# Last block of a linear attention: its scores taken ahead of the values of the block before, a moved root, and a 22nd weight buffer

## Chip, core and metric

One core of a Trainium2 chip runs the whole program. The metric is the device time in microseconds (us), the median over the executions shown; lower is better. Times inside the program are counted from the start of the profiled execution's span. All data is 32-bit floating point.

## What is computed

An input of 4 images, 128 channels, 64 x 64 positions passes two layers; each adds its result to the input. Layer 0 is an attention between all positions of an image (three fifths of the time; the change does not touch it). Layer 1 sees each image as 4096 tokens of 128 numbers, and has two parts:

```python
# attention that runs along the tokens: 8 heads of 128
kv = silu(einsum('btd,ed->bte', layernorm(t), W_kv));  k, v = kv[..., 0], kv[..., 1]
s  = einsum('hd,bthd->bth', q_proj, k)
m  = cummax(s, axis=1);  e = exp(s - m)
t  = t + (cumsum(e[..., None] * v, axis=1) / cumsum(e, axis=1)[..., None]).mean(axis=2)

# 64 experts, each of which chooses 8 tokens of each image
g = layernorm(t);  p = softmax(g @ gate_w.T + gate_b, axis=1)
topv, topi = top_k(p over the tokens, 8)            # for each expert
pooled = sum_k(topv * g[topi])
out = gelu(pooled @ weight1 + b1) @ weight2 + b2     # 64 pairs of matrices
t[topi] += out * topv
```

The experts' two weight arrays are the program's largest input: 64 units of 512 KB, that is one unit for every two experts in each of the two layers of the expert network.

## The kernel before, in words

Layer 1 goes over 32 blocks of 512 tokens (`NB = 32`; 8 blocks an image, 4 chunks of 128 tokens a block). The function `loop` (L1133) walks the blocks and issues, for block n:

- `keys` (L357): the keys of block n+1, eight matmuls into PSUM and eight Silu on ScalarE (L364, L365);
- `gate_stats` (L1002): mean and variance of the finished tokens of block n-1, on VectorE (L87, L88);
- `weights` (L898): transposes of the block's exponentials `es` (L902), a copy of them on ScalarE (L904), and on GpSimd their product with a triangular mask, in two halves `em` (L917); `weighted` (L924) then multiplies the halves with the inverse sums `rb` on VectorE (L926);
- `values` (L929): eight matmuls with the value weights `wvs` (L938) and eight Silu (L942);
- `gate_logits` (L1027), for an earlier block: a matmul `pl` (L1031), a copy with the bias on ScalarE (L1035) and the block's eight largest on VectorE (L1038, the `best()` of the code);
- `gate_norm` (L1007), for block n-1: a square root on ScalarE (L91), a reciprocal (L92), four normalisations (L96). `gate_turn` (L1020) later transposes these (L1023) and copies them (L1025);
- `totals` (L946): matmuls into `pt` (L954) and eight running additions into `before` on VectorE (L964);
- `score` (L835): the scores of block n+1, 16 matmuls (L839); `scan` (L845): two copies (L851), the running maximum (L856), a subtraction (L860), the exponential on ScalarE (L861), a copy of it on GpSimd (L866), the running sum (L871) and its reciprocal (L876); `spread` (L879): the reciprocal goes to DRAM and comes back spread over the partitions as `rb`, by six DMAs on SP's queue (L884, L891);
- `outputs` (L966): 128 matmul pairs into `po` (L974), 16 more with `before` and the reciprocal (L981), and the addition into the tokens `t` (L986).

TensorE's order is the order of this code, written out by hand (`manual_schedule`). The other engines' order is set by a scheduler at build time; `issue_after` holds an instruction behind another one there. Every engine then works off its own list in that order.

For the last block (n = 31, `not more`) there are no further keys or scores. There `gate_norm(30)` stands at the start of the block and runs on VectorE, `gate_turn(30)` and `gate_logits(30)` follow within the block.

After the loop comes the expert part, from L1219. The last block is normalised and its logits are made, the best tokens are chosen and pooled (L1315 to L1360), and then 16 groups of four experts run: `first` (L1362, matmuls L1367), `turn` (L1376), `second` (L1391, matmuls L1397), `gather`. At its end the results are added to `t` (L1480, L1487) and written (L1490).

The weights come through `load_units` (L1238), all on SP's queue. `NW = 21` units fit in at once: thirteen in a pool `fw` that is opened when the loop's buffers are closed, six in `room` (which held keys and transposed tokens), one each in `wks` and `wvs` (the key and value weights). Unit n lies in buffer n mod NW. The first 21 are issued as soon as their buffers are free; after that `first` and `second` issue two units each, into the buffers which they have just read. Two tiles of the gate, `xg` (L1010, normalised tokens) and `xt2` (L1024, their transpose), 2 KB a partition each, are in no unit's list.

Of the kernel before, what the change touches and what calls it, by code (L numbers as in the profile page):

```python
# [13 lines left out]
P = 128  # L14
# [4 lines left out]
def conv_attn_hybrid_kernel(  # L19
# [763 lines left out]
    GRP = BLK // H2  # L783
    EG = E // QG
    NB = B * NBLK
    NW = 21

    def layer1(pre, ready):

# [5 lines left out]
        with ExitStack() as kept, ExitStack() as l1:  # L795
# [46 lines left out]
                    )  # L842
                return pss

            def scan(n, pss):  # L845

                k = n % NBLK
                ss = sb.tile([P, BLK], F32, tag="ss", name=f"{pre}ss_{n}", bufs=1)
                for q in range(NPAIR):
                    half = bass.ts(q, BLK // NPAIR)  # L850
                    nc.vector.tensor_copy(  # L851
                        ss[:, half].rearrange("h (u s j) -> h s u j", u=2, s=2),
                        pss[:, half].rearrange("h (s u j) -> h s u j", u=2, s=2),
                    )
                mm = sb.tile([P, BLK], F32, tag="mm", name=f"{pre}mm_{n}", bufs=1)
                nc.vector.tensor_tensor_scan(  # L856
                    out=mm, data0=ss, data1=ss, op0=ALU.max, op1=ALU.max,
                    initial=state[:, 0:1] if k else LOWEST,
                )
                nc.vector.tensor_sub(ss, ss, mm)  # L860
                exp = nc.scalar.activation(ss, ss, AF.Exp).ins  # L861
                nc.gpsimd.tensor_copy(state[:, 0:1], mm[:, BLK - 1 : BLK])
                es = sb.tile([P, BLK], F32, tag="es", name=f"{pre}es_{n}")
                for q in range(NPAIR):
                    half = bass.ts(q, BLK // NPAIR)
                    nc.gpsimd.tensor_copy(  # L866
                        es[:, half].rearrange("h (s u j) -> h s u j", u=2, s=2),
                        ss[:, half].rearrange("h (u s j) -> h s u j", u=2, s=2),
                    )
                rr = sb.tile([P, BLK], F32, tag="rr", name=f"{pre}rr_{n}")  # L870
                nc.vector.tensor_tensor_scan(  # L871
                    out=rr, data0=ones.to_broadcast([P, BLK]), data1=ss,
                    op0=ALU.mult, op1=ALU.add, initial=state[:, 1:2] if k else 0.0,
                )
                nc.vector.tensor_copy(state[:, 1:2], rr[:, BLK - 1 : BLK])
                inverse = nc.vector.reciprocal(rr, rr).ins  # L876
                return es, rr, (exp, inverse)
# [68 lines left out]
            def totals(n, vs):  # L946

                pt = ps_t.tile([P, 2, GRP // 2, C], F32, tag="t", name=f"{pre}pt_{n}")
                for i, v in enumerate(vs):
                    for h in range(NH):  # L950
                        g, r = h % QG, h // QG
                        for u in range(2):
                            half = slice(u * H2, (u + 1) * H2)
                            nc.tensor.matmul(  # L954
                                pt[g * QW : (g + 1) * QW, u, i, :], ew[half, i, h, :], v[half, h, :],
                                start=(i == 0 and r == 0), stop=(r == NR - 1), skip_group_check=True,
                            )
                if n % NBLK == 0:
                    nc.vector.memset(before[:, 0, :], 0.0)
                else:  # L960
                    nc.vector.tensor_copy(before[:, 0, :], before[:, GRP, :])
                for x in range(GRP):
                    q, u, s = x // 4, x // 2 % 2, x % 2
                    nc.vector.tensor_add(before[:, x + 1, :], before[:, x, :], pt[:, u, 2 * q + s, :])  # L964

            def outputs(n, rr, aas, vs):  # L966
                po = ps_o.tile([P, 2, BLK], F32, tag="o", name=f"{pre}po_{n}")
# [29 lines left out]
            rden = lgp.tile([P, B // 2], F32, tag="rden", name=f"{pre}rden")  # L997

            total = lgp.tile([P, C], F32, tag="total", name=f"{pre}total")
            gmv, grs, xgs, gate_xts, picks, eighth, cts, lefts = {}, {}, {}, {}, {}, {}, {}, {}  # L1000

            def gate_stats(n):  # L1002
# [4 lines left out]
            def gate_norm(n, engine):  # L1007
                grs[n] = gp.tile([P, CPB], F32, tag="grs", name=f"{pre}grs_{n}", bufs=2)
                root = roots(grs[n], gmv[n])
                xgs[n] = gp.tile([P, CPB, C], F32, tag="xg", name=f"{pre}xg_{n}")  # L1010
                for c in range(CPB):
                    normalise(
                        engine, xgs[n][:, c, :], n * CPB + c, gmv[n][:, c, 0:1],
                        grs[n][:, c : c + 1],
                    )

                nc.gpsimd.tensor_copy(rs1[:, bass.ts(n, CPB)], grs[n])
                return root

            def gate_turn(n, ps):  # L1020
                ptr = ps.tile([P, CPB, P], F32, tag="kv", name=f"{pre}gtr_{n}")
                for c in range(CPB):
                    nc.tensor.transpose(ptr[:, c, :], xgs[n][:, c, :], ident)  # L1023
                gate_xts[n] = gp.tile([P, BLK], F32, tag="xt2", name=f"{pre}xt2_{n}")  # L1024
                nc.scalar.copy(gate_xts[n], ptr.rearrange("p c x -> p (c x)"))  # L1025

            def gate_logits(n, ps):  # L1027
# [105 lines left out]
            def loop():  # L1133
# [8 lines left out]
                for n in range(NB):  # L1142
# [2 lines left out]
                        ks = keys(n + 1, xt_of[n + 1], range(NH // 2), kss, ps_kv, pre)  # L1145
                    if n >= 1:
                        gate_stats(n - 1)
                    if not more:
                        gate_norm(n - 1, nc.vector)
                    if n + 2 < NB:  # L1150
                        xls = tokens(n + 2, xl_place)
                    if n == 0:
# [15 lines left out]
                    with ExitStack() as order:  # L1168
                        if k0 == 0:
                            with tc.issue_after(made[2][1]):  # L1170
                                order.enter_context(tc.issue_after(select(0)))
                        if 0 <= k0 < NBLK:
                            left = gp.tile([P, BLK], F32, tag="left", name=f"{pre}left_0_{k0}")
                            marked = pick_mark(0, k0, left)
                            if marked is not None:
                                order.enter_context(tc.issue_after(marked))
                        if 1 <= k0 <= NBLK:
                            order.enter_context(tc.issue_after(pick_turn(0, k0 - 1, ps_kv)))
                        if k0 == NBLK:
                            divisors(0)  # L1180
                        aas = weighted(ems, rbs)
                    vs, last = values(n, xt_of[n])
                    if n >= 2:
                        best = gate_logits(n - 2, ps_kv)
                    if not more:
                        gate_turn(n - 1, ps_kv)
                    if 1 <= k0 <= NBLK:
                        pick_add(0, k0 - 1)
                    with tc.issue_after(last):
                        if n >= 1 and more:  # L1190
                            gate_norm(n - 1, nc.gpsimd)
                        if n == 0 and ready:
                            roots(rs1[:, bass.ts(B - 1, NCH)], mv1[:, bass.ts(B - 1, NCH), :])
                    if n + 2 < NB:
                        copied[n + 2] = turned(n + 2, xls, xt_of[n + 2], ps_kv, pre)
                    totals(n, vs)
                    if not more:
                        best()
                        best = gate_logits(n - 1, ps_kv)
                    if more:  # L1200
                        pss = score(n + 1, ks)
                        with ExitStack() as order:
                            if 0 <= k0 < NBLK:
                                with tc.issue_after(copied[n + 2]):
                                    exp = pick_exp(0, k0)
                                order.enter_context(tc.issue_after(exp))
                            made = scan(n + 1, pss)
                        rbs = spread(n + 1, made[1])
                        if 0 <= k0 < NBLK:
                            with tc.issue_after(made[2][1]):  # L1210
                                pick_keep(0, k0)
                    outputs(n, rr, aas, vs)
                    if n >= 2:
                        best()

# [2 lines left out]

            l1.close()  # L1219
            pool = opener(l1, pre)  # L1220
            fwp = pool("fw", NW - 2 - ROOM)
            fo = pool("l2fo")
            fs = pool("l2fs", 2)
            ps_a = pool("l2a", 4, space=PSUM)
# [13 lines left out]
            def load_units(m):  # L1238
                for _ in range(m):
# [1 line left out]
                    if n >= len(units):  # L1241
                        return

                    if n % NW >= NW - 2:
                        w = wvs if n % NW == NW - 1 else wks.rearrange("d h e -> d (h e)")
                    elif n % NW >= NW - 2 - ROOM:
                        w = room[:, n % NW - (NW - 2 - ROOM), :]
                    else:
                        w = fwp.tile([P, FH + FC * C], F32, tag="fw", name=f"{pre}fw_{n}")
                    nc.sync.dma_start(out=w, in_=fw[units[n][0], units[n][1]])  # L1250
# [3 lines left out]
                w = unit_weights[layer, e // 2].rearrange("p (i x) -> p i x", i=2)[:, e % 2, :]  # L1254
                return w.rearrange("p (c o) -> p c o", c=FC) if layer else w

            load_units(NW)

            eos = fo.tile([P, B // 2, C], F32, tag="eo", name=f"{pre}eo")

# [29 lines left out]
            with tc.manual_schedule(engines={mybir.EngineType.PE}):  # L1290
# [25 lines left out]
                pool_tokens(0, total)  # L1316
                backs(2, nc.vector)
                best = gate_logits(NB - 1, ps_a)
                with tc.issue_after(copied[pre, NB - 1]):
                    backs(2, nc.scalar)  # L1320
                best()
# [233 lines left out]
```

## Time and profile before

| what | us |
|---|---|
| time, median of 3 runs | 2385.71 (2385.66 to 2388.26) |
| the profiled execution: its own time | 2384.92 |
| its span | 2383.2 |
| layer 0's last large matmul, L608 | starts 1444.4 |
| one block of the loop near its end (keys of 30 to keys of 31, 2187.48 to 2212.56) | 25.1 |
| last block's addition into the tokens, L986 | starts 2263.22 |
| first expert matmul, L1367 | starts 2289.87 |
| last unit of weights issued, L1250 | 2341.36 |
| first results ready to write | 2356.5 |

Busy shares of the span: TensorE 98%, VectorE 63%, ScalarE 51%, GpSimd 13%. These are averages over stages that have different limits. From the second of 40 slices of the span to about 2230 us TensorE is busy nearly without a break; in the last 150 us, where the change lies, it waits again and again, and the profile's timeline has to be read there row by row. Such a row gives the start, the time, the engine, the line, the operation, what it writes and reads, the tile's size and the count; in square brackets stands how long the engine had been idle before it and what ended this. The span is cut into 40 slices in the page's second part; the last three are the end of the loop and the experts:

```profile
ACT  5444444444443444443443335666666666666541
DMA packets 61765, 109.93 MB, mean 46 GB/s; under 512 B 10096, under 2 KB 35184, under 8 KB 61552
```

The first line is ScalarE's busy share in tenths by slice; the second sums the DMAs. A third of all bytes, 33.6 MB, are the 64 units of weights.

### The profile page before, as it was taken

What the parts mean: (1) busy time and instruction counts of PE and PEld (TensorE: products, weight loads), DVE (VectorE), ACT (ScalarE), POOL (GpSimd) and SP (SyncE); (2) the same over time, 40 slices, a digit from 0 to 9 for tenths busy, and PEclk for the clock granted to TensorE, in tenths of its full rate; (3) what the DMA queues carried; (4) which work ended last, traced back from release to release, by engine and by line L of the source; (5) the groups of instructions that cost most, each with busy time, mean ns of one, the idle gap of its engine ahead of it and who ended that gap; (6) DMA issues with size and microseconds to landing.
All of it is one profiled execution on the core that took longest, in us unless ns stands there. A gap on an engine that the chain in (4) does not pass through costs nothing.

```text
span 2383.2 us, 45629 instructions
## 1 busy us (share of the span) xinstructions
PE 2340.1 (98%) x19416; PEld 1554.0 (65%) x19416; DVE 1494.8 (63%) x2593; ACT 1208.1 (51%) x1639; POOL 304.2 (13%) x338
## 2 busy tenths in 40 slices
PE   7999999999999999999999999999999999999897
PEld 3567777677778677778777775555555555655554
DVE  6666666666656666655555556666666677776655
ACT  5444444444443444443443335666666666666541
POOL 0000000000000000000000002333343333333300
PEclk9999999999999999999999999999999999999999
DMA  3200110000100000020000000212112121112388
GB/s 83 75 23 19 41 39 1 17 13 23 49 25 1 23 7 23 18 52 1 1 1 1 1 1 19 55 38 55 38 38 55 38 54 39 38 38 55 118 307 322
DMA packets 61765, 109.93 MB, mean 46 GB/s; under 512 B 10096, under 2 KB 35184, under 8 KB 61552
## 3 DMA queue, kind: packets, MB, share of 16 engines
q1 hardware_dynamic: 57824, 101.22, 14.8%
q10 hardware_dynamic: 3728, 5.71, 0.7%
q8 instruction: 154, 2.52, 0.4%
q14 instruction: 59, 0.48, 0.1%
HBM read 85.40 MB, written 8.91 MB: 40 GB/s over the span
## 4 chain that ended last, share of the span: by engine, by line


## 5 line engine op out<-in xcount | busy, mean ns | idle before, releaser
L608 PE MATMUL av<-pr,am 64*128 64x512 f32 x4096 | 1057.2, 591 | 0.0
L587 ACT ACTIVATE pr<-sc 128x1024 f32<-128x1024 f32 x512 | 523.8, 1023 | 675.4 <-PE sc L583 606.7
L590 DVE TENSOR_TENSOR acc<-acc,pr 128x1024 f32<-128x1024 f32 x480 | 587.0, 1223 | 436.0 <-ACT pr L587 435.9
L608 PEld LDWEIGHTS av<-pr,am 64*128 64x128 f32 x4096 | 634.6, 187 | 260.4 <-issue 45.2
L583 PE MATMUL sc<-e,e 64*128 64x512 f32 x2048 | 618.9, 594 | 1.9 <-DMA e<-ee 1.9
L583 PEld LDWEIGHTS sc<-e,e 64*128 64x128 f32 x2048 | 317.3, 188 | 106.5 <-issue 19.5
L364 PE MATMUL pk<-room,wks 128*128 128x512 f32 x508 | 238.3, 607 | 2.0 <-ACT room L365 1.7
L938 PE MATMUL pv<-wvs,room 128*128 128x512 f32 x512 | 227.0, 596 | 2.5 <-ACT v L942 2.1
L942 ACT ACTIVATE v<-pv 128x512 f32<-128x512 f32 x256 | 152.7, 597 | 69.7 <-PE pv L938 69.7
L938 PEld LDWEIGHTS pv<-wvs,room 128*128 128x128 f32 x512 | 97.0, 191 | 121.9 <-issue 114.2
L926 DVE TENSOR_TENSOR em<-em,rb 128x1024 f32<-128x1024 f32 x64 | 78.4, 1224 | 154.4 <-DMA rb<-rd 154.4
L828 POOL MEMSET ew<- 128x1024 f32 x1 | 1.0, 952 | 1360.9 <-PE av L608 1360.9
L365 ACT ACTIVATE room<-pk 128x512 f32<-128x512 f32 x254 | 146.8, 597 | 54.4 <-PE pk L364 54.2
L364 PEld LDWEIGHTS pk<-room,wks 128*128 128x128 f32 x508 | 89.4, 189 | 107.6 <-issue 79.0
L917 POOL TENSOR_TENSOR em<-et,mask 128x1024 f32<-128x1024 f32 x64 | 122.6, 1937 | 79.0 <-ACT et L904 79.0
L96 POOL TENSOR_SCALAR xg<-t,gmv,grs 128x128 f32<-128x128 f32 x120 | 95.2, 806 | 287.3 <-DVE grs L92 209.4
L974 PEld LDWEIGHTS po<-v,em 64*64 64x64 f32 x4096 | 111.6, 133 | 29.1 <-DVE before L964 26.7
L974 PE MATMUL po<-v,em 64*64 64x128 f32 x4096 | 119.9, 271 | 1.9 <-issue 1.9
L876 DVE RECIPROCAL rr<-rr 128x512 f32<-128x512 f32 x32 | 107.3, 3353 | 1.1
L861 ACT ACT_TABLE_LOAD x24 | 30.8, 1283 | 121.1 <-DVE ss L860 121.1
L964 DVE TENSOR_TENSOR before<-before,pt 128x128 f32<-128x128 f32 x256 | 72.6, 284 | 9.6 <-PE pt L954 3.8
L871 DVE TENSOR_TENSOR_SCAN rr<-ones,state,ss 128x512 f32<-128x512 f32 x28 | 42.0, 1501 | 48.7 <-ACT ss L861 46.6
(203 smaller groups left out, 2031.5 us busy)
## 6 DMA issues: line engine op xcount, KB each, us to landing
rb<-rd SPq DMA_DIRECT2D x128, 256.0 KB
fw<-in_fw_dram SPq DMA_DIRECT2D x40, 512.0 KB
room<-in_fw_dram SPq DMA_DIRECT2D x18, 512.0 KB
t<-in_xtok_dram SPq DMA_DIRECT2D x32, 256.0 KB
e<-ee SPq DMA_DIRECT2D x63, 128.0 KB
x<-in_x_dram SPq DMA_DIRECT2D x12, 512.0 KB
e<-ee SPq DMA_DIRECT2D x63, 64.0 KB
out_dram<-t SPq DMA_DIRECT2D x8, 256.0 KB
```

Of the source, the lines that this page charges most:

```text
L96: i = engine.tensor_scalar(out=dst, in0=t[:, chunk, :], scalar1=mean, scalar2=rs, op0=ALU.subtract, op1=ALU.mult)
L364: nc.tensor.matmul(pk, wks[:, h, :], xt, start=True, stop=True)
L365: nc.scalar.activation(kss[h], pk, AF.Silu)
L583: nc.tensor.matmul(sc[:, u, :], e2[halves[u], p, :], e1[halves[u], :], start=True, stop=True)
L587: nc.scalar.activation(pr, sc, AF.Exp)
L590: added.append(nc.vector.tensor_add(acc, acc, pr).ins)
L608: nc.tensor.matmul(av, am[h, j, :], pr[h, u, :], start=(j == 0), stop=(j == NCH - 1))
L876: inverse = nc.vector.reciprocal(rr, rr).ins
L917: nc.gpsimd.tensor_tensor(em, eq.unsqueeze(2).to_broadcast([P, 2 * NH, H2]), mask.unsqueeze(1).to_broadcast([P, 2 * NH, H2]), ALU.mult,)
L938: nc.tensor.matmul(pv.rearrange("p h d -> p (h d)"), xt[:, bass.ts(2 * q + s, P)], wvs[:, bass.ts(m, BLK)], start=True, stop=True,)
L942: last = nc.scalar.activation(v[:, bass.ts(m, HPB), :], pv, AF.Silu).ins
L974: nc.tensor.matmul(po[s * H2 : (s + 1) * H2, u, q, :], aas[q][half, s, h, :], vs[2 * q + s][half, h, :], start=(q == 0 and h == 0), stop=F ...
```

## The change

Six edits, all in layer 1:

1. In iteration 30 the scores of block 31 are issued ahead of the values of block 30 (before: behind its totals).
2. In that iteration `scan` holds the exponential behind the last Silu of the values, and the running sum behind the last of the eight additions of `totals`.
3. In the last iteration `gate_norm(30)` is issued behind the last Silu of that block's own values; `gate_turn(30)` behind `totals`; `gate_logits(30)` behind `outputs`.
4. `xg` and `xt2` become the two halves of one tile, `gate_room` (4 KB a partition, as much as both had).
5. `NW` is 22: `gate_room` is the 22nd buffer. The pool `fw` keeps thirteen.
6. 21 units are issued at first as before; the 22nd, into `gate_room`, behind the logits of block 31.

```diff
-    NW = 21
+    NW = 22
...
-            def scan(n, pss):
+            def scan(n, pss, behind=()):
...
-                exp = nc.scalar.activation(ss, ss, AF.Exp).ins
+                with ExitStack() as order:
+                    for i in behind[:1]:
+                        order.enter_context(tc.issue_after(i))
+                    exp = nc.scalar.activation(ss, ss, AF.Exp).ins
...
+                with ExitStack() as order:
+                    for i in behind[1:]:
+                        order.enter_context(tc.issue_after(i))
+                    nc.vector.tensor_tensor_scan(
...
+            gate_room = gp.tile([P, 2 * BLK], F32, tag="gate_room", name=f"{pre}gate_room")
...
-                xgs[n] = gp.tile([P, CPB, C], F32, tag="xg", name=f"{pre}xg_{n}")
+                xgs[n] = gate_room[:, :BLK].rearrange("p (c d) -> p c d", c=CPB)
...
-                gate_xts[n] = gp.tile([P, BLK], F32, tag="xt2", name=f"{pre}xt2_{n}")
+                gate_xts[n] = gate_room[:, BLK:]
...
-                    if not more:
-                        gate_norm(n - 1, nc.vector)
...
+                    sooner = n + 2 == NB
+                    if sooner:
+                        pss = score(n + 1, ks)
                     vs, last = values(n, xt_of[n])
                     if n >= 2:
                         best = gate_logits(n - 2, ps_kv)
-                    if not more:
-                        gate_turn(n - 1, ps_kv)
...
                     with tc.issue_after(last):
                         if n >= 1 and more:
                             gate_norm(n - 1, nc.gpsimd)
+                        if not more:
+                            gate_norm(n - 1, nc.vector)
...
-                    totals(n, vs)
+                    added = totals(n, vs)
                     if not more:
+                        gate_turn(n - 1, ps_kv)
                         best()
-                        best = gate_logits(n - 1, ps_kv)
                     if more:
-                        pss = score(n + 1, ks)
+                        if not sooner:
+                            pss = score(n + 1, ks)
...
-                            made = scan(n + 1, pss)
+                            made = scan(n + 1, pss, (last, added) if sooner else ())
...
                     outputs(n, rr, aas, vs)
+                    if not more:
+                        best = gate_logits(n - 1, ps_kv)
...
-            fwp = pool("fw", NW - 2 - ROOM)
+            fwp = pool("fw", NW - 3 - ROOM)
...
+                    part = n % NW - (NW - 3 - ROOM)
+                    if part >= 0:
+                        w = (
+                            *(room[:, i, :] for i in range(ROOM)),
+                            wks.rearrange("d h e -> d (h e)"), wvs, gate_room,
+                        )[part]
...
-            load_units(NW)
+            load_units(NW - 1)
...
                 best = gate_logits(NB - 1, ps_a)
+                load_units(1)
```

## Prediction

> **What bounds the kernel now.** I read the busy rows first: TensorE is at nine tenths nearly to the end, but such an average hides single waits, and the edits reorder the last 150 us alone. There I read the timeline row by row, then the waits of SP's queue, then stretches. The timeline, 2230 to 2264 and at the first expert matmul:
>
> ```profile
> 2230.43 1.92 PE L839 MATMUL ps<-room,qz 128*32 128x512 f32 x16
> ...
> 2237.65 0.63 ACT L861 ACTIVATE ss<-ss 128x512 f32<-128x512 f32 x1
> ...
> 2240.04 3.35 DVE L876 RECIPROCAL rr<-rr 128x512 f32<-128x512 f32 x1
> ...
> 2243.56 1.28 ACT L91 ACT_TABLE_LOAD   x1
> ...
> 2245.91 0.30 ACT L91 ACTIVATE grs<-gmv,eps 128x4 f32<-128x4 f32 x1 [1.07 <-DVE gmv L88]
> 2246.23 1.28 ACT L942 ACT_TABLE_LOAD   x1
> ...
> 2248.17 3.70 PE L938 MATMUL pv<-wvs,room 128*128 128x512 f32 x8 [2.10 <-ACT v L942]
> ...
> 2250.88 1.23 DVE L926 TENSOR_TENSOR em<-em,rb 128x1024 f32<-128x1024 f32 x1 [3.20 <-DMA rb<-rd]
> ...
> 2254.21 1.23 DVE L926 TENSOR_TENSOR em<-em,rb 128x1024 f32<-128x1024 f32 x1
> ...
> 2258.85 3.27 PE L974 MATMUL po<-v,em 64*64 64x128 f32 x108 [1.86 <-issue]
> ...
> 2263.22 0.69 DVE L986 TENSOR_TENSOR t<-t,po 128x512 f32<-128x512 f32 x1 [4.62 <-PE po L981]
> ...
> 2289.87 1.04 PE L1367 MATMUL ph<-fw,pooled 128*4 128x512 f32 x8 [0.43 <-DVE pooled L1302]
> ```
>
> To be seen: the scores of block 31 end at 2232.35; a chain over VectorE, exponential, running sum, reciprocal and the trip through DRAM gives `em` only at 2254 and 2255.4; meanwhile ScalarE breaks off its Silus for a square root (two table loads round 2245.91). From L986 to the first expert matmul is a serial 26.65 us. From there the weights decide. SP's waits and two stretches (TensorE, PEld, VectorE, ScalarE, GpSimd busy, clock, DMA share, GB/s):
>
> ```profile
> SPq L1250 <- PE ph L1367: 20.1, 5, 16.3
> ...
> 2280.00:2290.00 10.00, 8.45 (x113) 6.62 (x113) 6.59 (x15) 2.70 (x5) 0.00 (x0) 1.00 0.13 50
> 2310.00:2320.00 10.00, 10.00 (x130) 6.11 (x129) 5.00 (x13) 5.05 (x14) 0.00 (x0) 1.00 1.03 406
> ```
>
> 21 units are loaded, the queue then waits 16.3 us for the first expert matmul, and from about 2300 to 2350 it runs at its ceiling of some 406 GB/s. At the end TensorE waits for `room` and `wks` (1.9, 1.1 and 1.1 us in the view of waits). So the end is set by (a) when the first expert matmul runs and (b) how many units are left then.
>
> **The change part by part**, against the profiled execution (2384.92 us, span 2383.2; the median is 0.79 above it). Times from here lack the leading 22.
>
> *Scores ahead (edits 1, 2).* 16 matmuls held TensorE from 30.43 to the next block of work at 32.28: 1.85. Moved to 20.65 they delay `values(30)` by that; the last Silu ends at 30.1, not 28.3. The last key's Silu ends at 21.45, when the seventh score would start, so it costs 0.2 at most. `po(30)` starts at 32.2 as before: what was behind it is now ahead, cost nothing. Gained: VectorE does L851, L856, L860 between 22.6 and 29.6, in the wait for `rb` (its second copy lies behind `em_0`, whose `rb` lands at 25.8). ScalarE, after the Silu at 30.1: table load 1.28, root 0.30, logits 0.68, table load 1.28, exponential 0.63, with gaps 34.4 instead of 38.28. On VectorE the eight additions follow the logits' maximum: 33.2 to 35.7 (8 x 0.316). Then running sum 1.50, reciprocal 3.35: done at 40.8, before 43.39, **2.6 earlier**. GpSimd has the four normalisations (3.13) first, until 35.5, so `es` is copied at 35.5 to 37.2, not 38.34 to 40.01.
>
> *The values of block 31 (edit 3).* TensorE finishes L981 at 37.0 and finds the exponentials almost there: transposes done 37.7, `et` 37.9, copy and table load to 40.1, first Silu 40.1 (before 42.94). Now no root interrupts: Silus 2 and 3 at once, then one each 0.86: last one ends at 46.0, before 52.51. Here the Trainium skill ("ScalarE: Activation LUTs", What ACT_TABLE_LOAD costs) puts a switch of tables at about 2.66 us, load and drain; the rows show 1.28 and no drain (43.56 + 1.28 = 44.84, root at 45.91 for want of variances). By the page the two switches removed are 5.3, by the rows 2.6 plus the 1.07 wait plus the root. I use the rows. Either way it isn't the sum: `values` is no longer what is late.
>
> *What is late next.* `em_1`. In block 30 it started 10.0 after the reciprocal's end (18.44 to 28.47): 40.8 + 10.0 = 50.8, ends 52.05 (before 55.44). The built order puts `em_0`, three normalisations, `em_1`, the fourth on VectorE (0.26 to 0.34 each), so the fourth ends at 52.4. `gate_turn(30)` is new ahead of `po`: TensorE waits for that fourth and starts `po` at 52.6. Additions of block 31: 52.9 to 55.5, hidden behind `po`. In the old trace `po` restarted at 58.85 with 108 of 128 and L986 came 4.37 later; all 128 take 0.59 more: L986 at 52.6 + 4.96 = 57.6, **5.6 earlier**. The old 1.86 of "issue" goes too: it came 3 us after `totals`, with weights in flight; now 4 us of waiting lie between, enough to fetch code.
>
> *The clock, which speaks against it.* `totals(31)` end at 48.1 and `po` starts at 52.6: TensorE does three transposes in 4.5 us. What that does, two stretches of the old trace (busy TensorE, clock, DMA share, GB/s) show:
>
> ```profile
> 2237.38:2240.79 3.41, 1.16 (x9) 1.00 0.32 126
> 2240.79:2244.20 3.41, 3.41 (x7) 0.50 0.00 0
> ```
>
> A stretch of 3.41 with 1.16 busy is followed by one at half the clock. The skill ("TensorE: Matmul & The Clock Gate", Part 1) says at least one idle window of about 3.4 us is needed, free-running; its table "Why this matters for your kernels" asks for "No PE-idle gaps >~3µs between matmul bursts". By the page's wording I would charge nothing unless a whole window falls into the gap; by the row a third busy is enough, so I charge it: on average some 2 us of `po` at half speed, **1.0 lost** (0 to 1.8). L986 then at 58.6, 4.6 earlier.
>
> *The tail.* `gate_logits(30)` now follows `po`: its two matmuls fit into the 0.75 between L981's end and the transposes of `t`. But on ScalarE its copy (0.68) and the seed stand ahead of the copies of transposes, and the next root waits for those: **0.4 later** (0 to 0.7). The table load at L1309 (1.28) goes; it was in ScalarE's slack.
>
> *Weights (edits 4 to 6).* The 13 `fw` loads start with L981's end and move with it. The 22nd follows them, 1.28 of transfer at about 76, in the queue's idle time before the first expert matmul at about 85.7: hidden. After that 42 units remain instead of 43, each freed buffer comes one unit earlier, and units land 1.28 apart in the stretch at the ceiling: **1.28 earlier**, as TensorE's waits there (4.1 us) exceed it. One tile in place of two adds waits to each normalisation of GpSimd, for its own work and TensorE's of a block ago, 20 us past: nothing. If these were late, GpSimd's queue (`es`, `em`) would pay; it is idle half of each block. SP's queue keeps its order around `rd` and `rb`; four `room` units and `wks` now start at 23.3 rather than 31.6, behind `rb(30)`, and are done by about 35, ahead of `rd(31)` at 40.8.
>
> Sum: -4.6 + 0.4 - 1.3 = **-5.5**; 2384.9 - 5.5 = 2379.4 in an execution like the profiled one, and from the median 2385.7 - 5.5 = **2380.2 us**.
>
> **Rivals.**
>
> *Most is given back (no measurable change).* A starved TensorE: weights now flow from 23 to 35, under `totals(30)` and `po(30)`, as they did under `po(31)` when it stood 2 us on "issue". One such stop at `po(30)` costs the path little (values have 2 us of slack against `em`), but a second in `po(31)`, 2.1, with the clock's 1.8 leaves 5.6 - 2.1 - 1.8 - 0.4 + 1.3 = 2.6: 2383.1. For it: that row. Against: `po(31)` is reached later after `totals` than before.
>
> *The 22nd unit brings nothing*, because the experts are bound by TensorE: 2381.5. Against it are the 4.1 us of waits for weights.
>
> *Slower.* One mechanism: code for TensorE held up by weights, at each of the four crossings between 30 and 58 plus one in the tail's transposes. Each is 2.1; three eat 6.4 of the 6.9 that the steps gain without the clock, so it decides from the fourth on the path: five with the clock's 1.0 and 0.4 for the tail give 2385.7 + 10.5 + 1.4 - 6.9 = 2390.7. Against: block 30 had 3.5 us of weights in flight at `po` without a stop.
>
> *It doesn't do what it says*: the built lists show each move, so only the sizes are open.
>
> **How the numbers follow.** Forecast, with gains between 4.8 and 8: 0.63. Given back: 0.23. No 22nd unit: 0.10 (half of it still past the bound, with less clock loss). Slower: 0.04. A difference under 0.2%, 4.8 us, is about what can't be told from none. So faster 0.68, same 0.28, slower 0.04. Range: below, no clock loss and no tail loss give 2378.8, and a selection that escapes the half clock which the old trace has at 2274.9 about 1 more, 2377.7; above, the first rival, 2383.1.
>
> **What would show it.** The exponential of block 31 near 34.4, no table load among the last Silus, their end at 46, L986 at 57.6 to 59, the first expert matmul at 84.5 to 86, the load into `gate_room` inside the idle stretch, the last unit issued near 2335.5. Wrong if `rb` of block 31 lands later than 10 us after its reciprocal, if `po(30)` shows "issue" and drags `es`, or if the clock is at half all through `po(31)`.

## The result, and the profile after

| | before | after |
|---|---|---|
| time, median of 8 executions each, same chip | 2386.1 (2384.91 to 2388.26) | 2380.34 (2377.78 to 2382.02) |
| ratio | | 0.9975, 95% interval 0.9966 to 0.9985 |
| the profiled execution's own time | 2384.92 | 2380.49 |
| first `rd` of block 30 issued (L884, now L892) | 2218.47 | 2217.95 |
| last block's addition into the tokens (L986, now L997) | 2263.22 | 2259.74 |
| first expert matmul (L1367, now L1389) | 2289.87 | 2286.61 |
| last unit of weights issued | 2341.36 | 2336.81 |

The changed kernel is faster: 5.8 us in the medians, 4.4 between the two profiled executions (4.5 in their spans). The latter splits into stages: L997 comes 3.48 earlier, the way from there to the first expert matmul is 0.22 longer, the stretch from that to the last unit is 1.29 shorter, and behind it nothing changes (41.83 and 41.86 to the end of the span). But 0.52 of the 3.48 was there already at the first `rd` of block 30, before the first edit acts (2218.47 and 2217.95 in the table); from there on L997 is 2.96 earlier. The timeline of the changed kernel, the rows that answer to those of before:

```profile
2233.47 0.63 ACT L866 ACTIVATE ss<-ss 128x512 f32<-128x512 f32 x1
...
2234.93 1.96 PE L985 MATMUL po<-v,em 64*64 64x128 f32 x59 [0.79 <-issue]
...
2237.07 3.35 DVE L884 RECIPROCAL rr<-rr 128x512 f32<-128x512 f32 x1
...
2240.93 1.57 ACT L950 ACTIVATE v<-pv 128x512 f32<-128x512 f32 x3
...
2246.17 0.60 ACT L950 ACTIVATE v<-pv 128x512 f32<-128x512 f32 x1 [0.26 <-PE pv L946]
...
2246.79 1.28 ACT L91 ACT_TABLE_LOAD   x1
...
2247.81 1.23 DVE L934 TENSOR_TENSOR em<-em,rb 128x1024 f32<-128x1024 f32 x1 [4.00 <-DMA rb<-rd]
...
2248.08 0.30 ACT L91 ACTIVATE grs<-gmv,eps 128x4 f32<-128x4 f32 x1
...
2250.04 1.23 DVE L934 TENSOR_TENSOR em<-em,rb 128x1024 f32<-128x1024 f32 x1
...
2251.57 0.33 PE L1036 MATMUL gtr<-ident,gate_room 128*128 128x128 f32 x1 [1.10 <-DVE gate_room L96]
...
2251.83 0.88 PE L985 MATMUL po<-v,em 64*64 64x128 f32 x22
...
2253.71 4.93 PE L985 MATMUL po<-v,em 64*64 64x128 f32 x106 [0.99 <-issue]
...
2259.74 0.69 DVE L997 TENSOR_TENSOR t<-t,po 128x512 f32<-128x512 f32 x1 [4.93 <-PE po L992]
...
2270.88 0.33 SPq L1271 DMA_DIRECT2D gate_room<-in_fw_dram  x1
...
2286.61 1.04 PE L1389 MATMUL ph<-fw,pooled 128*4 128x512 f32 x8 [0.43 <-DVE pooled L1323]
...
2336.81 0.33 SPq L1271 DMA_DIRECT2D wks<-in_fw_dram  x1
```

To be seen: the exponential of block 31 is 4.2 earlier than before, the Silus run through without a table load and end at 2246.77 instead of 2252.51, `em_1` is ready at 2251.27 instead of 2255.44. But `po` of block 31 runs badly: after 22 matmuls TensorE stands ("issue": the profile shows nothing that it waits for), and the other 106 take 4.93, where before 108 took 3.27. The stretches of the same execution (busy TensorE, its weight loads, VectorE, ScalarE, GpSimd, then clock, DMA share, GB/s) say why they are slow:

```profile
2250.52:2253.93 3.41, 1.36 (x31) 1.00 (x35) 3.18 (x9) 0.59 (x1) 0.00 (x0) 1.00 0.74 287
2253.93:2257.34 3.41, 3.41 (x72) 3.41 (x68) 0.81 (x3) 0.00 (x0) 0.00 (x0) 0.50 0.06 19
```

The clock is halved for one stretch of 3.41 from 2253.93: 4.93 against 3.2 for as many at full clock is 1.7 lost. And the load into `gate_room` goes out at 2270.88, while SP's queue has nothing else to do until the first expert matmul (`SPq L1271 <- PE ph L1389: 19.7, 5, 15.6` in the waits, the longest 15.6).

### The profile page after: what moved, and what is told of

The parts are those of the page before. It is cut to its first block, busy times and chain, and to the rows that moved or that the text cites. A ratio compares the mean times of both kernels' runs of the same rounds, so it can differ in the third digit from the quotient of the medians.

```text
span 2378.7 us, 45711 instructions
## 1 busy us (share of the span) xinstructions
PE 2338.3 (98%) x19416; PEld 1554.5 (65%) x19416; DVE 1495.5 (63%) x2593; ACT 1205.3 (51%) x1637; POOL 302.9 (13%) x338
## 4 chain that ended last, share of the span: by engine, by line
## 5 line engine op out<-in xcount | busy, mean ns | idle before, releaser
L608 PEld LDWEIGHTS av<-pr,am 64*128 64x128 f32 x4096 | 634.3, 187 | 260.8 <-issue 40.8
L96 POOL TENSOR_SCALAR gate_room<-t,gmv,grs 128x128 f32<-128x128 f32 x120 | 95.2, 805 | 281.8 <-DVE grs L92 193.7
L884 DVE RECIPROCAL rr<-rr 128x512 f32<-128x512 f32 x32 | 107.3, 3353 | 1.1
```

The lines of the kernel that those rows point to most:

```text
L96: i = engine.tensor_scalar(out=dst, in0=t[:, chunk, :], scalar1=mean, scalar2=rs, op0=ALU.subtract, op1=ALU.mult)
L608: nc.tensor.matmul(av, am[h, j, :], pr[h, u, :], start=(j == 0), stop=(j == NCH - 1))
```

## The experiments

Each run was timed beside the kernel before and left one profile; what each changes stands below the table. As executions differ by a microsecond or two before they reach block 30, places are compared as counted from the first `rd` of block 30, written `rd`(30); `po`(31) is `po` of block 31. "Half" marks a stretch at half clock that begins 1.4 to 2.2 us after the first expert matmul. The change of the median is against the kernel before as timed beside that run, its interval worked out from that of the ratio. A profile shows one execution only: for e3_scores, e5_gate_units and e8_both it is the fastest of its run, for e2_loop and e12_all_held the slowest (2381.57 against a median of 2378.12).

| run | median, change (95%) | `rd`(30) to L986 | stop in `po`(31) | L986 to first expert | first expert to last unit |
|---|---|---|---|---|---|
| before | | 44.75 | 1.86 | 26.65 | 51.49, half |
| changed kernel | -5.8 (-8.1 to -3.6) | 41.79 | 0.99 | 26.87 | 50.20, half |
| e2_loop | -5.3 (-7.6 to -3.3) | 42.70 | 1.22 | 27.26 | 51.79, half |
| e3_scores | +1.3 (-1.0 to +2.9) | 45.62 | 2.65 | 25.42 | 50.38 |
| e4_gate | -3.2 (-4.8 to -1.7) | 43.03 | 0.59 | 25.79 | 50.57 |
| e5_gate_units | -5.6 (-7.2 to -3.6) | 40.67 | none | 25.79 | 49.29 |
| e6_turn_late | -6.0 (-8.1 to -3.1) | 42.01 | 3.99 | 26.48 | 50.36, half |
| e7_held | -9.9 (-12.6 to -6.2) | 38.42 | none | 27.42 | 48.82 |
| e8_both | -9.3 (-12.2 to -5.5) | 37.60 | none for code | 26.48 | 49.20 |
| e9_before_held | -5.0 (-7.2 to -3.3) | 42.79 | none | 25.42 | 51.84, half |
| e10_loop_held | -8.9 (-12.4 to -5.7) | 38.77 | none | 25.79 | 51.49, half |
| e11_warm | -8.2 (-10.3 to -4.5) | 39.22 | none | 26.67 | 48.92 |
| e12_all_held | -8.3 (-12.2 to -5.7) | 41.46 | none | 27.46 | 50.29, half |

### The change taken apart

**e1_units**: edits 4 to 6 on the kernel before.

```diff
-    NW = 21
+    NW = 22
...
-                xgs[n] = gp.tile([P, CPB, C], F32, tag="xg", name=f"{pre}xg_{n}")
+                xgs[n] = gate_room[:, :BLK].rearrange("p (c d) -> p c d", c=CPB)
```

> Before with the 22nd unit alone (edits 4 to 6), the loop of the last block as before. Theory of the prediction: the first expert matmul stays where it was (2289.87, within 0.5), the load into gate_room lands in the idle time of the queue ahead of it, and the stretch from the first expert matmul to the last unit issued shrinks from 51.49 to about 50.2; time 1.3 us less (0.8 to 1.8). Rival (the experts are bound by TensorE, the queue's gain ends in waits elsewhere): no difference, 0 +- 0.5, with TensorE's waits for weights at the end shorter by 1.3 and its last matmul where it was.

Measured: 6259.45 us (6255.39 to 6262.44). In the old order `gate_norm(30)` stands at the start of block 31, ahead of `gate_turn(29)`. Two tiles of one name keep these apart; one fixed tile doesn't, and block 29's gate then reads block 30's tokens. The program tests at its end whether each expert has chosen no more than eight tokens, and otherwise computes everything again by a general path; that is the rest of the 6259. One row of the timeline shows the exchange, TensorE standing 6.5 us for VectorE's normalisations of block 30 before it may transpose "block 29":

```profile
2245.57 1.15 PE L1024 MATMUL gtr<-ident,gate_room 128*128 128x128 f32 x4 [6.51 <-DVE gate_room L96]
```

That equal logits of two blocks are counted twice, and so fail that test, is read from the code and was not tried by itself. What follows: edit 4 needs edit 3, which puts `gate_norm(30)` behind `gate_turn(29)`. The unit has to be measured on top of it.

**e2_loop**: edits 1 to 3, with 21 units.

```diff
-    NW = 22
+    NW = 21
```

(against the changed kernel, with edits 4 to 6 taken back)

> Before with the reordered last block alone (edits 1 to 3), 21 units. Theory: L986 some 3.5 us earlier (59.7), tail 0.2 longer, the units' stretch as before at 51.5: 3.3 us less (2.5 to 4.6). If the order and the units add up, this and the 22nd unit alone together give the whole change's 4.6 to 5.8. Rival (the whole gain is the order's, the units bring nothing): 4.5 us less or more.

Measured: 2380.06, as good as the whole change, as the rival had it. But the profile has a stretch from first expert to last unit of 51.79, like before's 51.49; two medians of executions that each spread over more than 4 us don't resolve 1.3.

**e3_scores**: edits 1 and 2 alone. **e4_gate**: edit 3 alone.

```diff
+                    sooner = n + 2 == NB
+                    if sooner:
+                        pss = score(n + 1, ks)
                     vs, last = values(n, xt_of[n])
```

> Before with edits 1 and 2 alone: scores of block 31 ahead, exponential behind; the square root stays between the Silus of block 31 and gate_turn(30) stays ahead of the values. Theory A (em_1 was made late by the exponential, the values with them; the earlier exponential carries the gain): exponential near 33.5 to 34.5, reciprocal ends near 40.5, em_1 ends near 51.3, last Silu of block 31 at 49.5 to 50.5 in spite of the root, so po can start at 51.5 without the fourth normalisation's wait: L986 at 57 to 60, 3 to 5 us less, as much as the whole reordering. Rival B (the root between the Silus is what is late): last Silu still near 52, po from there, L986 near 62, 1 us less or nothing.

```diff
-                    if not more:
-                        gate_norm(n - 1, nc.vector)
...
                     with tc.issue_after(last):
+                        if not more:
+                            gate_norm(n - 1, nc.vector)
```

> Before with edit 3 alone: gate_norm, gate_turn and gate_logits of block 30 behind the values, the scores and the exponential of block 31 where they were. Theory A: last Silu ends near 49 but em_1 still ends at 55.4, the fourth normalisation at 55.8 and gate_turn stands ahead of po, so po starts no earlier: 0 to +1 us, L986 at 63 to 64. Rival B (the values are what is late): L986 2 to 3 us earlier, 2 to 3 us less.

Measured: the scores alone +1.3 (no gain), the gate alone -3.2, both -5.3. Theory A fails in both. In e3_scores the exponential is at 2232.71 and `em_1` ready at 2250.24, as early as A had it; but the root still splits the Silus, the last of which ends 34.1 after `rd`(30), as late as before (34.0), which is rival B's account; and TensorE has work of its own left. The timeline of e3_scores on TensorE from the last values on:

```profile
2250.51 1.02 PE L1040 MATMUL pl<-xt,gws 128*128 128x512 f32 x2
2251.36 0.60 PE L1032 MATMUL gtr<-ident,xg 128*128 128x128 f32 x4
2251.89 2.03 PE L960 MATMUL pt<-v,ew 64*32 64x128 f32 x128
2253.85 1.13 PE L1040 MATMUL pl<-xt,gws 128*128 128x512 f32 x2
2254.91 0.87 PE L983 MATMUL po<-v,em 64*64 64x128 f32 x20
2258.43 3.27 PE L983 MATMUL po<-v,em 64*64 64x128 f32 x108 [2.65 <-issue]
```

Logits, transposes, totals and again logits fill 4.4 us between the values and `po`; that chain, not `em_1`, was late, and a longer stop took the rest. In e4_gate it is the other way round:

```profile
2253.75 1.01 PE L1023 MATMUL gtr<-ident,xg 128*128 128x128 f32 x4 [2.18 <-DVE xg L96]
2254.69 0.88 PE L974 MATMUL po<-v,em 64*64 64x128 f32 x22
2256.16 4.84 PE L974 MATMUL po<-v,em 64*64 64x128 f32 x106 [0.59 <-issue]
```

The values are done early (last Silu 2249.38), and TensorE waits for the normalisations behind the late `em_0`. From `rd`(30), `po` starts 2.0 earlier than before and its stop is 1.3 shorter (counted from the last matmul ahead of it to the next), of which a stretch at half clock from 2256.0 takes 1.6 back (4.84 for 106 matmuls). Two chains meet at `po`; either edit alone leaves the other one late. (The profile of e3_scores is of its fastest execution, 2382.33, whose tail and experts met no half clock.)

### The stop, and what it waits for

**e6_turn_late**: the changed kernel with the transposes of the gate behind `po`.

```diff
                     added = totals(n, vs)
                     if not more:
-                        gate_turn(n - 1, ps_kv)
                         best()
...
                     outputs(n, rr, aas, vs)
                     if not more:
+                        gate_turn(n - 1, ps_kv)
```

> The changed kernel with gate_turn(30) moved behind outputs(31), so that po(31) no longer waits for the fourth normalisation. Theory (the wait for the fourth normalisation and its low clock cost the 2.5 us between em_0 and po): po starts at 49.1 after em_0, its second half after em_1 at 51.3, L997 at 56 to 57.5 instead of 59.74; on the tail 0.3 to 0.5 is given back, since gate_turn's copy and its logits now stand ahead of the transposes; 2 to 3 us less than the changed kernel. Rival (po is bound by the fetch of TensorE's code while weights are in flight, so an earlier start only makes a longer stop): a stop of 2 to 3 us inside po, L997 at 58.5 or later, gain under 1 us.

**e7_held**: the changed kernel with the loads of one part of `room`, of `wvs` and of the first `fw` units waiting for the last value matmul of `po`(31). **e8_both**: both edits.

```diff
-                    nc.sync.dma_start(out=w, in_=fw[units[n][0], units[n][1]])
+                    load = nc.sync.dma_start(out=w, in_=fw[units[n][0], units[n][1]]).ins
+                    if n < NW and (part < 0 or part in (0, ROOM + 1)):
+                        tc.add_manual_dep(load, mixed.name, ...)
```

> The changed kernel with the loads of room 0, wvs and the first fw units held until the last value matmul of po(31) has run, so that no weights are in flight while TensorE goes through totals and po of block 31; they are still loaded before the first expert matmul, in the queue's idle time. Theory (the issue stop in po(31) is code for TensorE held up by weights): the stop of 1.0 to 1.3 us in po(31) falls to 0.3 or less, L997 1 us earlier, 0.5 to 1.5 us less than the changed kernel. Rival (the fetch is late for itself, weights or not): the stop stays at 1 us or more, no difference, or a loss where the later weights push out the first expert matmul.

> The two edits together: gate_turn(30) behind outputs(31), and the loads held behind the value matmuls of po(31). If the wait for the normalisation and the code held up by weights are separate costs, po runs from em_0 and em_1 without a stop, L997 at 54.5 to 56, 3.5 to 5 us less than the changed kernel (about 2376). If the earlier start only moves the stop, or the stop isn't from the weights: no better than gate_turn behind outputs alone.

TensorE in the timeline of e6_turn_late, of e7_held and of e8_both:

```profile
2248.85 1.08 PE L985 MATMUL po<-v,em 64*64 64x128 f32 x26
2253.93 4.57 PE L985 MATMUL po<-v,em 64*64 64x128 f32 x102 [3.99 <-issue]
```

```profile
2250.66 3.72 PE L985 MATMUL po<-v,em 64*64 64x128 f32 x128
...
2254.45 0.33 SPq L1274 DMA_DIRECT2D room<-in_fw_dram  x1
```

```profile
2248.34 1.08 PE L985 MATMUL po<-v,em 64*64 64x128 f32 x26
2250.58 3.06 PE L985 MATMUL po<-v,em 64*64 64x128 f32 x102 [1.15 <-issue]
```

In e6_turn_late `po` starts 2.6 earlier from `rd`(30) than in the changed kernel and goes on 0.6 later: the rival, with a stop of 3.99 where it had 2 to 3. In e7_held, with the weights away until 2254.45, all 128 matmuls run through in 3.72. The 1.15 in e8_both ends with `em_1` (ready at 2250.46 by its row on VectorE): a wait for data. So the stop comes from the weights. The DMA records of queue q8, which the page's third part lists thus for the changed kernel, show how:

```profile
q8 instruction: 154, 2.52, 0.5%
```

These are 154 packets of 16 KB. That they are TensorE's program is inferred: the 19416 matmuls and 19416 weight loads of that page make 252 to a packet, and TensorE's stops end 1.3 to 1.6 behind one, as the last two columns show. Around `po`(31) one of them counts:

| | first weights issued | that packet starts (took) | `po` goes on |
|---|---|---|---|
| before | 2251.90 | 2256.54 (0.93) | 2258.85 |
| changed kernel | 2246.17 | 2251.35 (1.08) | 2253.71 |
| e2_loop | 2245.61 | 2250.72 (1.08) | 2253.17 |
| e3_scores | 2250.70 | 2255.91 (0.95) | 2258.43 |
| e4_gate | 2248.94 | 2253.77 (1.07) | 2256.16 |
| e5_gate_units | 2247.08 | 2251.12 (1.08) | no stop |
| e6_turn_late | 2245.96 | 2251.51 (1.07) | 2253.93 |
| e7_held | 2254.45 | 2247.63 (1.26) | no stop |

With weights in flight the packet starts 4.0 to 5.6 us after they were issued, and TensorE, where it stood, goes on 1.3 to 1.6 after the packet's end; in e7_held, without them, the packet starts while TensorE is still in `totals`. Counted from the start of `totals`(31), it starts 3.4 to 4.8 later in the seven profiles with weights in flight and 1.2 to 2.6 later in the six where they are held. The stop is what remains of that time when TensorE gets there: 2 to 4 us where it comes straight from `totals` (before, e3_scores, e6_turn_late), 0 to 1.2 where it first waits for the normalisations.

The gain of e7_held in the median is 4.1 us more than the changed kernel's, larger than the stop in that one profile (0.99). The two weren't timed side by side and the intervals of their changes overlap, but e6_turn_late, which was timed beside e7_held, is 3.9 above it. From `rd`(30) to L997 the two profiles differ by 3.37: the stop with its edges 1.26, the half clock in `po` 1.7, an earlier start 0.3. Whether the hold also keeps the clock up, or the changed kernel's profile only met it there, one profile each doesn't tell.

**e9_before_held**: the hold on the kernel before, nothing else.

> Before, order and 21 units unchanged, with the hold alone: the loads of room 0, wvs and the first fw units wait for the last value matmul of po(31). Theory (every order of the last block pays for weights in flight at po(31), and the old order's 1.86 to 2.1 of stop is that price): no stop in po(31), L986 near 61.2, 2 us less than before (1 to 4), about 2383.5. Then the reordering is worth 6 to 7 us on top of the hold (against 2375.8 for both with the 22nd unit). Rival (holding the loads gains elsewhere, by the loads' order or their later start): the gain is the same 4.6 as the changed kernel had from it, about 2381.

Measured: -5.0, nearer to the rival's 4.6 than to theory's 2 and outside its 1 to 4, while its profile shows theory's 1.96 at L986 and no stop:

```profile
2254.62 4.06 PE L974 MATMUL po<-v,em 64*64 64x128 f32 x128
```

Another 1.23 lie in the tail (25.42 against 26.65, where the profile of before has a stretch at half clock), against it 0.35 in the stretch of the units, together 2.8. The remaining 2 us aren't placed: single profiles of before and of this run differ by 1.5 already at block 30, and how long the stop of before is in its other executions no profile here shows. What holds is that the hold gains without the reordering, and that the reordering gains with the hold: `rd`(30) to L986 goes from 42.79 to 38.77 in e10_loop_held, and the median by 3.9.

**e12_all_held**: all 21 first loads held, those ahead of block 30's `po` too.

```diff
-                    if n < NW and (part < 0 or part in (0, ROOM + 1)):
+                    if n < NW - 1:
```

> The changed kernel with all 21 first loads held until the last value matmul of po(31), those of four parts of room and wks too, which otherwise start at 2222 to 2224, under totals and po of block 30. Theory (the stop of about 1 us in po(30) is the same thing, but lies beside a wait: em_1 of block 31, not TensorE, sets po(31)): no stop in po(30), L997 within 0.3 us of the run with fewer loads held (38.42 after the first rd of block 30), the loads end near 2282, just ahead of the first expert matmul, time within 0.7 us of 2375.78. Rival (the stop at po(30) is on the path through the values): 1 us less. Second rival (21 units don't fit between 2254 and the first expert matmul): first expert matmuls wait for weights, 1 us more or worse.

Measured: 2378.12 (2375.02 to 2381.57), no gain, and 2.3 above e7_held where the theory allowed 0.7. The stop in `po`(30) is gone, the Silus of block 31 end 1.1 earlier than in e7_held counted from `rd`(30) (28.01 against 29.09), and `em_1` is where it was (33.12 against 33.03): off the path, as the theory had it. But L997 is 3 us later than in e7_held, and the stretches of e12_all_held show why in this execution, its slowest:

```profile
2248.02:2251.43 3.41, 1.54 (x61) 0.94 (x45) 3.10 (x6) 0.90 (x2) 0.19 (x1) 1.00 0.28 62
2251.43:2254.84 3.41, 2.79 (x45) 2.57 (x49) 3.14 (x10) 0.58 (x1) 0.00 (x0) 0.50 0.08 22
2254.84:2258.25 3.41, 3.41 (x72) 3.41 (x68) 0.41 (x2) 0.00 (x0) 0.00 (x0) 0.50 0.01 2
```

TensorE reached its wait for `em` sooner and stood longer, and two stretches of half clock followed: `po` took 6.53 instead of 3.72. Whether this also sets the median, no profile here shows.

### The 22nd unit

**e5_gate_units**: edits 3 to 6. **e10_loop_held**: edits 1 to 3 with the hold and 21 units.

> Before with edits 3 to 6: the gate's steps of block 30 behind the values, and the 22nd unit; scores and exponential where they were. Measured against the run with edit 3 alone (2382.13, 0.13% under before). Theory of the prediction (the queue at its ceiling sets the end, so one unit less to load is 1.3 us): about 2380.8, 0.19% under before, and the stretch from the first expert matmul to the last unit issued 1.3 shorter in a profile with the same clock there. Rival (the 22nd unit brings nothing, as 2380.34 for the whole change against 2380.06 for the reordering alone has it): within 0.5 us of 2382.1.

> Edits 1 to 3 with the hold, 21 units: the changed kernel with the hold (2375.78) less its 22nd unit alone, with no stop in po(31) in either, so that the unit is seen without that noise. Theory: 1.3 us more than 2375.78 (0.8 to 1.8), about 2377.1, first expert matmul the same, the stretch from it to the last unit issued 1.3 longer. Rival (the 22nd unit brings nothing): within 0.5 of 2375.8.

Measured: e5_gate_units 2380.11, 2.0 under e4_gate; e10_loop_held 2377.03, 1.25 above e7_held. Both point the way of the theory, and neither is decided by medians of 5 to 19 executions. The profiles decide it, once runs of the same clock are put side by side (last column of the table): with 21 units the stretch takes 50.38 and 50.57 without a half-clock stretch at its start, 51.49 to 51.84 with one; with 22 units 48.82 to 49.29 and 50.20 to 50.36. The unit is worth 1.4 in either state, the half clock at the first expert matmuls 1.2. e2_loop against the changed kernel in the medians (0.3 the wrong way as they stand, 0.5 the right way as changes in the table) is within their spread.

### The clock

**e11_warm**: e7_held with eight matmuls that nobody reads in three of TensorE's waits.

```diff
                     added = totals(n, vs)
                     if not more:
+                        warm(3, ps_kv, 0)
                         gate_turn(n - 1, ps_kv)
```

> The changed kernel with the hold, and eight matmuls whose results nobody reads put into three waits of TensorE: three ahead of gate_turn(30), three ahead of gate_turn(31), two ahead of the last transposition of row. Clock theory (a free-running stretch of 3.41 us with less than about 1.9 us of matmul is often followed by one at half clock, and these cost some executions 1 to 1.7 us each): no half-clock stretch between 2245 and 2295 in the profile, 0.5 to 1.2 us less than 2375.78 in the median and a narrower spread. Rival (the half clock falls into slack, or the fillers delay what follows them): no difference, or up to 0.5 us more.

Measured: 2377.72, 1.9 above e7_held. The clock stays full from 2245 to 2295 as meant, but two other things were paid. Each such matmul of 32-bit numbers is two in the records, so three of them took 2.84 instead of 1.4, and `po` starts 0.8 later from `rd`(30) than in e7_held (33.6 to 34.4). And from the first output to the end of the span it is 28.75, where all others have 26.7 to 26.9: with 32 more matmul and weight-load records the last packet of q8 starts at 2372.24 (1.36), and TensorE's closing instructions, two of which lie 0.15 apart in e7_held (2371.10 and 2371.25), lie 3.95 apart here (2371.10 and 2375.05). The second comes 1.45 after the end of that packet, within the 1.3 to 1.6 seen at `po`(31). What the half clock costs in the median isn't settled by this run.

The best version is e7_held, the changed kernel with the weights held: 2375.78 (2373.59 to 2378.30), ratio 0.9961 to the kernel before (0.9947 to 0.9974); e8_both is as good.

## Why the prediction was right

The time was forecast at 2380.2, measured were 2380.34. Step by step:

- *Scores ahead*: right. `values(30)` is 1.4 later in the trace's own time and 1.9 counted from `rd`(30) (1.85 forecast), its last Silu ends at 29.85 (30.1), the exponential is at 33.47 (34.4), the reciprocal ends at 40.42 (40.8). e3_scores shows that this alone gains nothing, which the forecast had not asked.
- *The values*: the first Silu at 40.93 (40.1), the last ends at 46.77 (46.0), no table load among them. The 0.8 is the stop of 0.79 in `po`(30), named in the first rival and costing nothing, as e12_all_held shows. On the price of a switch the rows stay right against the Trainium skill ("ScalarE: Activation LUTs", What ACT_TABLE_LOAD costs): the Silu ends at 2246.77, a load of 1.28 follows from 2246.79, the root at 2248.08, with no drain between.
- *What is late next*: right, `em_1` at 50.04 (50.8), then the normalisation, `po` at 51.83 (52.6).
- *The stop*: wrong. "The old 1.86 of "issue" goes too", since 4 us of waiting would be enough to fetch code. It came again with 0.99, and with 0.59 and 1.22 in e4_gate and e2_loop; only in e5_gate_units it was gone. The wait was 2.9, from 2248.96 to 2251.83, not 4. It shortens the stop, but the code packet comes some 5 us behind the weights, and these now start at 2246.17 instead of 2251.90. This is the first rival's mechanism at half its price. What the forecast held against it, that `po`(30) ran without a stop under weights, has another explanation in the DMA records of before: the packet ahead of that `po` started at 2230.41, before the four loads at 2231.55.
- *The clock*: the right sign, mis-sized: 1.0 charged, 1.7 lost. The rows were the better guide than the Trainium skill ("TensorE: Matmul & The Clock Gate", Part 1), which asks for an idle window. Counting matmul records between 2228 and 2300 in before, the changed kernel and all runs but e1_units, 20 stretches at full clock were followed by half clock; they were 0 to 1.82 of 3.41 busy, and only one was idle. Of 34 stretches as little busy, 14 were not followed by it; under 1.5 us, one of 12 was not.
- L997 by these: 3.48 earlier instead of 4.6. Start of `po` 0.8 ahead of the forecast, stop 1.2 behind with its edges, clock 0.7 behind: 1.1 together, as found. But 0.5 of those 0.8 is the head start at `rd`(30); without it L997 gained 2.96, and the forecast of `po` was 1.6 too good.
- *The tail*: 0.22 later (0.4). Where neither has a stretch at half clock, the new order takes 25.79 and the old 25.42: 0.37.
- *The weights*: 1.29 earlier (1.28), 1.4 at the same clock. One tile for two is not free of order, as e1_units shows, but in this change the order was right for it. The four `room` units started at 2222.84, as forecast; `wks`, which the forecast let start earlier with them, had been issued at 2223.31 before and came at 2224.89 now.
- *Sum*: between the two profiled executions -4.4, forecast -5.5; the medians have -5.8 (-8.1 to -3.6). So the time came out nearer than the working deserved: the stop and the clock in `po` cost about 1.9 more than forecast, an earlier start, half a microsecond of it from ahead of block 30, gave back 0.8, and the medians are kinder than the pair of profiles by 1.4. That the forecast time was met within 0.2 is luck; the order of steps and the gain of the unit are not.
- *Slower*: didn't happen. Two crossings paid 0.79 and 0.99, and only the second on the path.

## What to carry to other kernels

Where TensorE stands on "issue" within a long unrolled stretch, look at what transfers were issued some microseconds earlier: bulk loads that aren't needed yet can hold up the code of the engine that everyone waits for, and making them wait for a late matmul gained as much here as the whole reordering (4 to 5 us each). Where two chains meet at one instruction, shorten both or neither: +1.3 and -3.2 alone, -5.3 together. And before stages of two profiles are subtracted, sort them by the clock that they ran at: one stretch of 3.41 at half clock costs up to 1.7, as much as many an edit brings.

## What the runs showed of the hardware that was not expected

- TensorE's code comes, by these traces, in packets of 16 KB over the DMA engines (queue q8). With units of 512 KB in flight the packet for `po`(31) started only 4.0 to 5.6 us after these were issued, and TensorE stood for up to 3.99 us (e6_turn_late); with the weights held it never stood there for code (e7_held, e8_both, e9_before_held, e10_loop_held, e11_warm, e12_all_held).
- A half-clock stretch needs no idle one before it: 19 of 20 followed on stretches with 0.92 to 1.82 of their 3.41 us busy with matmuls.
- A few instructions more can lengthen a program's very end by 1.9 us: in the profile of e11_warm, with 32 more, TensorE's last instructions came 1.45 after the end of a code packet, and the rest waited for them.
